# Two paths behind one branch: which block of code lies next to the branch at the end of a segment-attention kernel

## The chip, the cores and the metric

The kernel runs on one core of one Trainium2 chip. A core has five engines with a queue of instructions each: PE (TensorE, matmuls), DVE (VectorE), ACT (ScalarE), POOL (GpSimd) and SP (SyncE, which here only starts transfers). The metric is the device time of one execution in microseconds (us), the median of five runs.

## The reference

16384 tokens of 256 features come with a segment number from 0 to 7 each. Attention runs inside every segment, a linear map follows, then a normalisation of each column over all tokens, a ReLU and the residual. Cut to what matters:

```python
q, k, v = feat @ Wq, feat @ Wk, feat @ Wv          # 32, 32 and 256 columns
starts = jnp.searchsorted(bids, jnp.arange(B))
pos = jnp.arange(N) - starts[bids]
qp, kp, vp = (pad(q), pad(k), pad(v))              # .at[bids, pos].set, 8 x 3072 slots
scores = jnp.einsum('bld,bmd->blm', qp, kp)
scores = jnp.where(mask[:, None, :], scores, NEG)
rp = jnp.einsum('blm,bmd->bld', softmax(scores), vp)
t = rp[bids, pos] @ Wt
tn = (t - t.mean(axis=0)) / jnp.sqrt(t.var(axis=0) + EPS) * gamma + beta
return feat + relu(tn)
```

## The kernel before, in words

The segment numbers of this input are not sorted, so only some tokens own a slot of a segment. The kernel has two paths for this.

The **short path** is `segment_attention_bn_kernel` itself. It holds for segments of at most 768 owners (`FW = FT * P`, six tiles of 128 rows) and for softmax sums within limits. It lists the owners of each segment, gathers their rows, projects them, and attends segment by segment; two switches on the segments' tile counts (L1371) choose the code of each half. From L1403 on it writes the output: sixteen groups of 1024 tokens are read, get the rows of the tokens that own no slot added by matmuls (L1483, L1488) and an add (L1497) or a copy (L1495), and are written by a DMA that ACT starts (L1501). Beside this, POOL writes the owners' rows token by token with indirect DMAs (L1516), in the arms of a third switch (L1529) that POOL alone decides. L1439 to L1441 write `bad`: zero where the short path holds.

The **long path** is `any_lengths` (L41). It computes the whole thing anew for segments of any length, with loops, and stands behind the branch at L1548.

Each engine has its own copy of this control flow. At the end of the short path every engine loads `bad` into a register (L1542) and compares it with zero at L1548. For this input `bad` is zero, so no engine runs the long path. In the compiled order of before, the code of one engine then reads:

```
L1542 TensorLoad bad
L1548 CompareAndBranch
L1548 (the short block: waits, on POOL the counter update, then UnconditionalBranch)
L77 ... L526  any_lengths, ending in L1548 UnconditionalBranch
L1581 the final block
```

The short block is what an engine runs where the long path is not taken. It holds the waits that bring the engines' semaphores to the same state as behind the long path: DVE, ACT and PE wait for their own last instruction and for their load of `bad`; POOL waits for the semaphores of its eight queues of indirect DMAs and then resets them (the ISA instruction, `INC_SWDGE_SEM` in the trace); SP waits for the semaphores of the DMAs that SP and ACT started, the last output groups among them. The unconditional branch at its end leads past the long path into the final block (L1581 in the trace): SP checks all semaphores, every engine drains and reports to a barrier that POOL gathers, the semaphores are cleared, a second barrier follows, and the execution ends.

The trace calls conditional and unconditional branches alike `COMPARE_BRANCH`. On the engines that the change touches, the long path between the short and the final block has 753 instruction rows on PE, 662 on DVE, 396 on ACT, 441 on POOL and 280 on SP (a row can stand for several instructions).

Of the kernel before, what the change touches and what calls it, by code (L numbers as in the profile page):

```python
# [531 lines left out]
def segment_attention_bn_kernel(  # L532
# [44 lines left out]
    with ExitStack() as short:  # L577
# [964 lines left out]
    again = nc.values_load(  # L1542
        bad[0:1, 0:1],
        min_val=0,
        max_val=P * TT + 1,
        skip_runtime_bounds_check_because="a count",
    )
    with tc.If(again > 0, preferred_fallthrough_block=False):  # L1548
        any_lengths(tc, feat, bids, wq, wk, wv, wt, gamma, beta, out)


# [33 lines left out]
```

## Time and profile before

| | us |
|---|---|
| median of 5 runs | 409.54 |
| the five runs | 411.44, 407.35, 412.80, 409.54, 404.53 |
| the profiled execution, its own time | 408.98 |
| its span, first to last instruction | 407.2 |
| mean granted clock of PE in it | 0.779 |
| busy: PE, DVE, POOL, ACT | 292.5, 262.7, 169.1, 109.0 |
| last matmul, as recorded | 389.4 |
| last copy on ACT (L1495), start | 392.7 |
| last output transfer's semaphore, seen by SP | 401.1 |

The page gives shares over the whole span; what the change touches lies in the last 4% of it, so that the views by line and by stretch of time are the ones to read. In them "q" behind an engine's name (POOLq, PEldq) is its sequencer, whose waits, branches and drains are not counted as busy. A line of such a view holds the count of an instruction, its least, median and longest duration in ns, and the start of the first and of the last one in us.

### The profile page before, as it was taken

The page shows a single profiled execution, that of the slowest core. Times are in us where ns is not written, and L with a number is a line of the kernel's source. Part 1 is how long each engine was busy: PE and PEld are TensorE (multiplying, and loading weights), DVE is VectorE, ACT ScalarE, POOL GpSimd, SP SyncE. Part 2 cuts the span into 40 slices and gives each one's busy share as a digit, 9 for nine tenths or more (in the row PEclk, how much of TensorE's full clock was granted, in tenths as well). Part 3 has the DMA queues.
Part 4 walks back from the last instruction along what each step waited for, and adds up shares of the span by engine and source line. Part 5 has one row for each costly group of instructions (what it writes and reads, how often), then busy time and mean ns, then how long its engine had stood idle before and what let it go on. Part 6 is the DMA issues. An engine that isn't in the chain of part 4 may idle for free.

```text
span 407.2 us, 4145 instructions
## 1 busy us (share of the span) xinstructions
PE 292.5 (72%) x1139; PEld 180.0 (44%) x1139; DVE 262.7 (65%) x776; ACT 109.0 (27%) x208; POOL 169.1 (42%) x181
## 2 busy tenths in 40 slices
PE   1669596820599989849798969996596878569920
PEld 0336364510357758616585657763132333123300
DVE  8973799415478853658787236467998975269710
ACT  8414433100333443314213422442011211022100
POOL 3425057778132050067875720000114077743740
PEclk9979699875689999968989989999555555555555
DMA  4101022020211220221032102177799997965642
GB/s 108 39 7 57 2 60 79 22 60 0 77 29 46 78 68 4 82 51 50 18 117 81 42 0 70 22 272 238 277 399 402 386 384 295 346 248 200 263 159 100
DMA packets 20905, 53.34 MB, mean 131 GB/s; under 512 B 6606, under 2 KB 13344, under 8 KB 16746
## 3 DMA queue, kind: packets, MB, share of 16 engines
q1 hardware_dynamic: 11493, 25.06, 17.4%
q10 hardware_dynamic: 2421, 16.83, 10.3%
q0 software_dynamic: 6928, 10.81, 8.8%
q14 instruction: 48, 0.39, 0.4%
q8 instruction: 15, 0.25, 0.3%
HBM read 26.67 MB, written 29.92 MB: 139 GB/s over the span
## 4 chain that ended last, share of the span: by engine, by line
PE 50%; DVE 18%; issue 12%; DMA 8%; another core or an unknown queue 4%; ACT 3%; DVEq 0%; SPq 0%; ACTq 0%
PE po L1008 20%; PE pv L953 8%; PE pf L1488 7%; PE pqk L934 5%; DMA work<-in_r_feat 5%; PE s L967 4%; DMA out<-work 3%; PE px L922 2%; PE pf L1483 2%; DVE work L1497 2%; DVE tk L1013 1%; DVE upto L887 1%; DVE work L941 1%; DVE py L1456 1%
## 5 line engine op out<-in xcount | busy, mean ns | idle before, releaser
L1008 PE MATMUL po<-work 128*128 128x257 f32 x394 | 101.8, 407 | 9.9 <-ACT work L972 4.8
L1008 PEld LDWEIGHTS po<-work 128*128 128x128 f32 x394 | 77.9, 204 | 27.3 <-ACT work L972 6.5
L836 POOL DMA_INDIRECT xs<-in_r_feat,idx x48 | 50.5, 1052 | 79.7 <-issue 40.7
L1516 POOL DMA_INDIRECT out<-tk,idx x48 | 47.3, 985 | 45.5 <-DVE tk L1458 22.1
L836 POOL DMA_INDIRECT reads_r<-reads_of,idx x48 | 53.5, 1115 | 19.3 <-issue 15.0
L953 PE MATMUL pv<-wvt,work 128*128 128x256 f32 x164 | 40.8, 400 | 24.3 <-issue 19.9
L953 PEld LDWEIGHTS pv<-wvt,work 128*128 128x128 f32 x164 | 31.5, 197 | 33.0 <-issue 22.4
L1483 PE MATMUL pf<-y,hot 48*128 48x256 bf16 x128 | 27.7, 390 | 20.1 <-issue 8.4
L1497 DVE TENSOR_TENSOR work<-work,pf 128x512 f32<-128x512 f32 x40 | 26.0, 682 | 23.7 <-remote 13.9
L1488 PE MATMUL pf<-work,ident 128*128 128x256 f32 x64 | 39.1, 714 | 3.1 <-DMA work<-in_r_feat 3.1
L1012 DVE RECIPROCAL rdens<-po 128x1 f32<-128x1 f32 x39 | 6.2, 164 | 52.9 <-PE po L1008 32.7
L972 ACT ACTIVATE work<-s,mask 128x512 f32<-128x512 f32 (+2 forms) x62 | 32.6, 600 | 18.5 <-PE s L967 10.1
L997 ACT ACTIVATE sq<-tk 128x256 f32<-128x256 f32 x39 | 16.3, 417 | 57.9 <-DVE tk L1013 47.1
L1483 PEld LDWEIGHTS <-hot 48*128 48x128 bf16 x128 | 7.2, 104 | 47.4 <-issue 47.3
L967 PE MATMUL s<-work 32*128 32x512 f32 (+2 forms) x124 | 24.9, 597 | 2.8 <-ACT work L972 2.8
L957 ACT COPY work<-pv 128x512 f32<-128x512 f32 (+1 forms) x21 | 12.0, 576 | 48.0 <-remote 21.4
L1495 ACT COPY work<-pf 128x512 f32<-128x512 f32 x16 | 9.4, 585 | 54.7 <-PE pf L1488 38.8
L934 PE MATMUL pqk<-work,wqk 128*128 128x512 f32 (+2 forms) x52 | 23.1, 589 | 0.4 <-issue 0.4
L922 PE MATMUL px<-ident,xs 128*128 128x128 f32 x82 | 15.3, 288 | 9.8 <-issue 4.6
L1488 PEld LDWEIGHTS pf<-work,ident 128*128 128x128 f32 x64 | 16.0, 310 | 12.4 <-issue 9.1
L998 DVE SCALAR_TENSOR_TENSOR acc<-sq,reads_r,acc 128x256 f32<-128x256 f32 x39 | 18.8, 482 | 1.2 <-ACT sq L997 0.7
L1488 PE MATMUL pf<-f,ident 128*128 128x256 f32 x32 | 19.5, 714 | 0.0
(241 smaller groups left out, 371.9 us busy)
## 6 DMA issues: line engine op xcount, KB each, us to landing
work<-in_r_feat SPq DMA_DIRECT2D x14, 1024.0 KB
out<-work ACTq DMA_DIRECT2D x14, 1024.0 KB
t_rows<-tk SPq DMA_DIRECT2D x3, 768.0 KB
t_rows<-tk SPq DMA_DIRECT2D x4, 512.0 KB
f<-in_r_feat SPq DMA_DIRECT2D x2, 1024.0 KB
out<-f ACTq DMA_DIRECT2D x2, 1024.0 KB
eb<-edge_of SPq DMA_DIRECT2D x16, 96.0 KB
t_rows<-tk SPq DMA_DIRECT2D x4, 256.0 KB
```

Source lines behind the costliest of these rows:

```text
L836: nc.gpsimd.indirect_dma_start(out=dst, out_offset=None, in_=table, in_offset=bass.IndirectOffsetOnAxis(ap=ind, axis=0), bounds_check=n - ...
L922: nc.tensor.transpose(px[:, ts(t, P)], xs[:, b * FT + t0 + t, ts(h, P)], ident)
L934: nc.tensor.matmul(pqk[:, 0:w], wqk[:, h, :], xT[:, h, own_c], start=(h == 0), stop=(h == DH - 1),)
L953: nc.tensor.matmul(pv[:, t, :], xT[:, h, ts(t0 + t, P)], wvt[:, h, :], start=(h == 0), stop=(h == DH - 1),)
L967: nc.tensor.matmul(s[:, i, 0:w], k[g, t // 4, :], q[g, c : c + w], start=True, stop=True)
L972: nc.scalar.activation((pr_b if c else pr_a)[:, t, 0:w], s[:, i, 0:w], AF.Exp, bias=mask[:, m : m + 1],)
L998: nc.vector.scalar_tensor_tensor(acc[:, 1, :], sq, reads_r[:, one], acc[:, 1, :], ALU.mult, ALU.add)
L1008: nc.tensor.matmul(po, pr[:, t, ts(r, P)], v[:, t, :], start=(t == 0), stop=(t == T - 1))
L1483: nc.tensor.matmul(pfs[k][:, u, :], hot[r, c, i + u, :], y3[r, :], start=True, stop=not on_pe,)
L1488: nc.tensor.matmul(pfs[k][:, u, :], ident, f_bufs[k % IOB][:, i + u, :], start=False, stop=True,)
L1497: nc.vector.tensor_add(two, two, pfs[k])
L1516: w = nc.gpsimd.indirect_dma_start(out=out, out_offset=bass.IndirectOffsetOnAxis(ap=idx[:, at : at + 1], axis=0), in_=y, in_offset=None, b ...
```

## The change

The order of the blocks behind the branch at L1548 is turned round, and the block gets a name:

```diff
-    with tc.If(again > 0, preferred_fallthrough_block=False):
+    with tc.If(again > 0, preferred_fallthrough_block=True, label="long"):
         any_lengths(tc, feat, bids, wq, wk, wv, wt, gamma, beta, out)
```

The compiled order of one engine becomes:

```
L1542 TensorLoad bad
L1548 CompareAndBranch
L77 ... L526  any_lengths, ending in L1548 UnconditionalBranch
L1548 (the short block: waits, on POOL the counter update, then UnconditionalBranch)
L1581 the final block
```

The instructions themselves and their waits are the same on all five engines; everything ahead of the branch keeps its order.

## The prediction

> **What bounds the kernel now.** I read the chain of waits first, then the end stretch by stretch, then the two lines whose code is rearranged. The chain, cut to 380 us and later:
>
> ```profile
> 386.45 0.58 ACT work L1495
> 387.04 5.65 another core or an unknown queue
> 392.69 0.02 issue
> 392.71 0.58 ACT work L1495
> ```
>
> The last computed thing is a copy on ACT at 392.7, which waited for PE (PE's recorded matmuls end at 389.4, but its semaphore comes at 392.7). Nothing ahead of this is touched, so the change can only move what lies between the first branch of an engine and the end of the span at 407.2. The stretches after 393, with engines' busy time, PE clock, DMA share and GB/s in their last columns:
>
> ```profile
> 393.00:396.00 3.00, 0.00 (x0) 0.00 (x0) 0.00 (x0) 0.30 (x1) 0.25 (x1) 0.50 0.67 254
> 396.00:399.00 3.00, 0.00 (x0) 0.00 (x0) 0.00 (x0) 0.00 (x0) 0.00 (x0) 0.50 1.02 421
> 399.00:402.00 3.00, 0.00 (x0) 0.00 (x0) 0.00 (x0) 0.00 (x0) 0.00 (x0) 0.50 0.13 49
> 402.00:407.20 5.20, 0.00 (x0) 0.00 (x0) 0.00 (x0) 0.00 (x0) 0.00 (x0) 0.50 0.02 5
> ```
>
> The last output groups land by about 401; then 6 us pass in which no engine computes and hardly a byte moves. What fills them stands in the sequencers' lines of the branch (L1548) and of the final block (L1581, cut to 390 us and later):
>
> ```profile
> L1548 SPq EVENT_SEMAPHORE  x9: 17/17/700, 354.9 to 401.3; - x9
> L1548 POOLq EVENT_SEMAPHORE  x6: 17/30/43, 393.8 to 396.5; - x6
> L1548 SPq COMPARE_BRANCH  x2: 33/369/705, 353.4 to 401.4; - x2
> L1548 PEldq COMPARE_BRANCH  x2: 98/1912/3727, 384.7 to 393.0; - x2
> L1548 DVEq COMPARE_BRANCH  x2: 41/52/64, 389.8 to 390.4; - x2
> ...
> L1548 POOLq COMPARE_BRANCH  x2: 38/47/56, 393.7 to 398.1; - x2
> L1548 ACTq COMPARE_BRANCH  x2: 33/44/55, 395.3 to 395.6; - x2
> ...
> L1548 POOLq INC_SWDGE_SEM  x1: 1418/1418/1418, 396.6 to 396.6; - x1
> ```
>
> ```profile
> L1581 SPq EVENT_SEMAPHORE  x14: 17/28/28, 403.9 to 407.1; - x14
> L1581 POOLq EVENT_SEMAPHORE  x4: 17/17/17, 406.4 to 407.1; - x4
> L1581 POOLq DRAIN  x3: 46/109/5137, 401.2 to 406.9; - x3
> L1581 SPq DRAIN  x3: 7/7/7, 404.7 to 406.6; - x3
> L1581 DVEq DRAIN  x2: 10/29/48, 393.6 to 406.6; - x2
> L1581 PEldq DRAIN  x2: 8/36/65, 396.8 to 406.7; - x2
> L1581 ACTq DRAIN  x2: 8/44/80, 401.4 to 406.6; - x2
> ```
>
> Two branches per engine: the first is the comparison, which falls into the short block; the second jumps over the long path. From the second to the first instruction of the final block pass 3.2 us on DVE (390.4 to 393.6), 3.8 on PE (393.0 to 396.8, with the branch's own 3.7), 5.8 on ACT (395.6 to 401.4), 3.1 on POOL (398.1 to 401.2), 2.5 on SP (401.4 to 403.9). A branch into code that is at hand costs far less: POOL's first leads to its first wait in 0.1 us (393.7 to 393.8). So the long jump is a stall of 2.5 to 5.8 us, worst while the output groups move. SP and POOL take theirs after their waits for the DMAs, the others while they'd wait anyway. SP reports to the barrier at 404.7 to 404.8. POOL is last: its drain of 5.1 us runs from 401.2 to 406.3, and the rest takes 407.2 - 406.3 = 0.9.
>
> **The change, part by part.** In the new order the comparison itself makes the long jump, ahead of the waits, and the branch behind the waits is a short one.
>
> DVE, PE: the jump starts 0.6 us earlier on DVE (389.8) and 8.3 earlier on PE (384.7). Both reported at 393.6 and 396.8 and wait for the barrier until 406.5. Worth nothing. If PE's jump held up queued matmuls it would show on ACT, but PE's matmuls were running on from the queue across the branch at 384.7.
>
> ACT: the jump starts at 395.3 instead of 395.6. With the same 5.8 it lands at 401.2; two waits (0.2 from the comparison to the second branch) and a short branch (0.1) give 401.5, against 401.4. It reports some 5 us ahead of POOL's end: cost nothing, and still nothing if POOL gains 3.
>
> SP: the jump starts at 353.4, under the output traffic; its waits then hold it until 401.4 as before. The 2.5 behind them becomes 0.1; its checks in the final block take 403.9 to 404.7, 0.8. It reports at 401.4 + 0.1 + 0.8 = 402.3, 2.5 earlier. SP starts no DMA behind the branch, so nothing is queued behind the jump.
>
> POOL: the jump starts at 393.7 and ends at 393.8 plus its stall. By the range of rows that is 396.3 to 399.6; I take 3.7, PE's row, because PE's jump starts at 393.0, nearest in time and traffic: 397.5. Before, POOL's last waits opened only at 396.4, so 2.6 us of the stall lie under waits that were there anyway and 1.1 sticks out. Then six waits (four took 393.8 to 394.1, two 0.2: 0.5 in all), the counter update (1.4) and the short branch (0.1): the drain begins at 397.5 + 0.5 + 1.4 + 0.1, about 399.6 with the fractions, 1.6 before 401.2. With a stall of 2.5 it would be 398.4 (2.8 earlier); with ACT's 5.8 it is 401.7 (0.5 later).
>
> The unknown is the drain, seen once at this length. The other two on POOL took 0.11 and 0.05 us. I take 5.1 from its start: everything that it could wait for by name was done (POOL's transfers by 396.5, the update by 398.0, output by 401.1), and no other event stands near 406.3. Then POOL ends at 399.6 + 5.1 = 404.7 and the span at 405.6. The bounds: zero, whereupon SP is last (402.3), and an end that hangs on the update instead.
>
> Sum: 407.2 - 1.6 = 405.6 of span, 408.98 - 1.6 = 407.4 for that execution. The median of the runs is 0.6 above it: 407.9. The case's own range is a gain of 2.8 to a loss of 0.5, 406.7 to 410.0 on the median.
>
> Were the second branch no longer at hand when reached (the short block's end and the final block parted by a border of what is loaded), POOL would pay a second stall, 3.1 by its row: 1.5 slower. The two blocks are neighbours and the waits and update last about 2 us, so I only let it widen the range.
>
> The Trainium skill weighs against the whole account: "Advanced Engine Details and Errata", Control Flow Timing, gives about 51 ns for a branch and 108 for a comparison. By these the rearrangement would be worth 0.1 us and the time would stay; the gaps of 2.5 to 5.8 above contradict it for distant targets. And "VectorE: DVE Perf Modes", The DRAIN you can't avoid, calls the drains at a kernel's ends a constant 12 ns or so on all engines; by it SP would set the end and the gain would be that of the third rival below, but POOL's record of 5.1 us differs.
>
> **The rivals.**
>
> *The drain ends a fixed time after the counter update (slower).* The update resets the counters of the queues of 51 indirect DMAs, and the drain's end is 406.3 - 398.0 = 8.3 us after it. If work begun there is what the drain waits for, the time goes by the update's end: 397.5 + 0.5 + 1.4 = 399.4, plus 8.3 is 407.7, a loss of 1.4, or 410.9 on the median; with ACT's stall, a loss of 3.5 (413.0). It turns against the change as soon as POOL's jump takes over 2.3 us (396.6 - 0.5 - 393.8), below every jump seen. For it: the first drains follow no such update and are short. Against: the update is recorded as done.
>
> *The drain ends by something that the change doesn't move.* No difference: 409.5. For it: 5.1 us have no visible cause. Against: I find no event there.
>
> *The drain is short when it begins earlier, or is no work at all.* It would have to shrink below 402.3 - 399.6 = 2.7; then SP's 402.3 plus 0.9 ends the span at 403.2, a gain of 4.0: 405.5. For it: the other two drains. Against: nothing visible held this one back.
>
> **How the numbers follow.** Forecast 0.55, slower by the update 0.20, no difference 0.12, short drain 0.13. All lie between 405.5 and 413.0. The five runs spread by 8.3 us, 2% of the median, which is what a measurement can tell from no change; with a standard deviation of some 3.3 their median is uncertain by 1.25 * 3.3 / 2.24 = 1.8. I add most of that to the shorter cases: 404.2 to 411.4, leaving out the slow end of the first rival. Over 2% either way means 8.2 us: to gain it nearly all behind 399 would have to vanish, to lose it two or three stalls would have to stack on one engine. 0.94 within, 0.03 each side.
>
> **What would show it.** Right: in the lines of L1548 one long gap behind the comparison of each engine, at 354 on SP and 394 on POOL, and the second branch 0.1 before the final block; SP's checks ending 0.9 after its last DMA wait; POOL's drain near 399.6, 5.1 long. A drain still ending 8.3 after the update, or shrunk to less than 2.7, names the rival. Wrong from the ground: a long gap behind the second branch as well, or PE's last semaphore later than 392.7 relative to its matmuls.

## The result and the profile after

| | before | after |
|---|---|---|
| median of the runs, us | 409.26 (94 runs, 401.31 to 421.50) | 406.37 (52 runs, 399.00 to 419.23) |
| the profiled execution, us | 408.98 | 408.30 |
| its span, us | 407.2 | 406.4 |
| mean granted clock of PE | 0.779 | 0.773 |

The ratio after to before is 0.9921 with an interval of 0.9890 to 0.9951: of 409.26 us that is a gain of 3.2 us, between 2.0 and 4.5. It is real, and within 2%. Comparisons set aside disturbed executions, more than 1.5% above a kernel's fastest; as these times spread by 5%, the ratios of the experiments, with some ten runs each, hang on a few runs, and where such a ratio and the medians disagree, both are told.

The two profiled executions differ by 0.8 us of span, a quarter of that gain. They have to be compared piece by piece. First the branch (L1548) in the kernel after; a line has the count, the least, median and longest duration in ns, and the first and last start in us:

```profile
L1548 SPq EVENT_SEMAPHORE  x9: 17/17/17, 361.3 to 403.1; - x9
L1548 POOLq EVENT_SEMAPHORE  x6: 17/30/43, 398.5 to 399.0; - x6
...
L1548 SPq COMPARE_BRANCH  x1: 6/6/6, 356.5 to 356.5; - x1
L1548 PEldq COMPARE_BRANCH  x1: 4870/4870/4870, 385.7 to 385.7; - x1
L1548 DVEq COMPARE_BRANCH  x1: 70/70/70, 392.2 to 392.2; - x1
L1548 POOLq COMPARE_BRANCH  x1: 62/62/62, 395.7 to 395.7; - x1
L1548 ACTq COMPARE_BRANCH  x1: 60/60/60, 397.8 to 397.8; - x1
L1548 POOLq INC_SWDGE_SEM  x1: 1418/1418/1418, 399.1 to 399.1; - x1
```

The long gap now follows the comparison (a jump is counted here from the end of the branch to the engine's next instruction; on PE it is the branch's own time): 395.7 to 398.5 on POOL, 356.5 to 361.3 on SP, 397.8 to ACT's first wait at 403.5, 392.2 to 395.2 on DVE, and 4.9 us on PE. Each engine shows one branch instead of two, so the second has no record in the trace; its cost is read from the final block (L1581, cut to 385 us and later):

```profile
L1581 POOLq DRAIN  x3: 46/109/5052, 400.5 to 406.1; - x3
L1581 SPq DRAIN  x3: 7/7/7, 403.9 to 405.8; - x3
L1581 PEldq DRAIN  x2: 8/8/8, 395.4 to 405.9; - x2
L1581 DVEq DRAIN  x2: 10/14/17, 395.4 to 405.9; - x2
L1581 ACTq DRAIN  x2: 8/8/8, 403.7 to 405.8; - x2
```

POOL's update ends at 399.1 + 1.4 = 400.5 and its drain starts at 400.5, so no stall is left behind the waits. The drain ends at 400.5 + 5.05 = 405.6, and that is again the last thing: SP is ready at 404.0, ACT at 403.7. The end of the chain of waits (start, us, what) has another piece:

```profile
387.97 7.08 another core or an unknown queue
395.05 0.02 issue
395.07 0.59 ACT work L1495
```

ACT's last copy starts at 395.07, 2.36 later than before. The recorded matmuls end at 390.3, 0.9 later, and the copy comes 4.8 after them where it came 3.3 after them in the trace of before. So this execution was behind by 2.4 when its end began, and made up 3.1 from there. ACT's copy isn't the best mark, though, as POOL's last events do not follow from it directly. POOL's last indirect writes, before and after:

```profile
L1516 POOL DMA_INDIRECT out<-L,idx x3: 983/984/984, 389.7 to 392.3; - x3
```

```profile
L1516 POOL DMA_INDIRECT out<-L,idx x3: 985/987/987, 390.6 to 393.2; - x3
```

From the end of the last one (393.25 before, 394.21 after) to the end of the span pass 13.95 and 12.20 us: 1.75 less.

### The profile page after: what moved, and what is told of

Read it like the earlier page. It is cut to its first block, busy times and chain, and to the rows that moved or that the text cites. A ratio compares the mean times of both kernels' runs of the same rounds, so it can differ in the third digit from the quotient of the medians.

```text
span 406.4 us, 4140 instructions
## 1 busy us (share of the span) xinstructions
PE 297.8 (73%) x1139; PEld 183.1 (45%) x1139; DVE 263.2 (65%) x776; ACT 109.3 (27%) x208; POOL 166.9 (41%) x181
## 4 chain that ended last, share of the span: by engine, by line
PE 56%; DVE 17%; issue 10%; another core or an unknown queue 5%; DMA 5%; ACT 3%; ACTq 0%; DVEq 0%; SPq 0%
PE po L1008 24%; PE pv L953 10%; PE pf L1488 7%; PE pqk L934 4%; PE s L967 4%; DMA work<-in_r_feat 3%; PE pf L1483 3%; PE px L922 3%; DMA out<-work 2%; DVE work L1497 2%; DVE tk L1013 1%; DVE py L1456 1%; DVE tk L1458 1%; PE pc L867 1%
## 5 line engine op out<-in xcount | busy, mean ns | idle before, releaser
L1008 PE MATMUL po<-work 128*128 128x257 f32 x394 | 104.6, 415 | 13.0 <-issue 6.4
L1008 PEld LDWEIGHTS po<-work 128*128 128x128 f32 x394 | 79.4, 208 | 31.3 <-issue 10.2
L836 POOL DMA_INDIRECT reads_r<-reads_of,idx x48 | 51.2, 1066 | 20.9 <-issue 15.6
L953 PEld LDWEIGHTS pv<-wvt,work 128*128 128x128 f32 x164 | 32.5, 203 | 28.4 <-issue 22.8
L967 PE MATMUL s<-work 32*128 32x512 f32 (+2 forms) x124 | 26.9, 641 | 2.6 <-ACT work L972 2.6
L922 PE MATMUL px<-ident,xs 128*128 128x128 f32 x82 | 16.4, 302 | 9.4 <-ACT work L945 3.7
L934 PE MATMUL pqk<-work,wqk 128*128 128x512 f32 (+2 forms) x52 | 22.2, 568 | 0.4 <-issue 0.4
```

Of the source, the lines that this page charges most:

```text
L836: nc.gpsimd.indirect_dma_start(out=dst, out_offset=None, in_=table, in_offset=bass.IndirectOffsetOnAxis(ap=ind, axis=0), bounds_check=n - ...
L922: nc.tensor.transpose(px[:, ts(t, P)], xs[:, b * FT + t0 + t, ts(h, P)], ident)
L934: nc.tensor.matmul(pqk[:, 0:w], wqk[:, h, :], xT[:, h, own_c], start=(h == 0), stop=(h == DH - 1),)
L953: nc.tensor.matmul(pv[:, t, :], xT[:, h, ts(t0 + t, P)], wvt[:, h, :], start=(h == 0), stop=(h == DH - 1),)
L967: nc.tensor.matmul(s[:, i, 0:w], k[g, t // 4, :], q[g, c : c + w], start=True, stop=True)
L1008: nc.tensor.matmul(po, pr[:, t, ts(r, P)], v[:, t, :], start=(t == 0), stop=(t == T - 1))
```

## The experiments

The forecast left open what the long jump costs POOL once it stands ahead of the waits, and what the drain's end depends on. The theory is that POOL loses only what of its jump sticks out behind the landing of its last indirect write, and that its drain counts from its own start. The diffs below show the lines that differ from the named kernel, with a line or two around them; "..." marks what is left out.

**The order of before, with POOL late.** Two fills of a tile of 128x768 on POOL, and a copy on DVE that POOL waits for, stand between the last write and the load of `bad`. If the wait opens when a transfer lands, POOL has time to spare there in the old order:

```diff
+    tc.no_sync_barrier()
+    scr = bad_pool.tile([P, FW], F32, name="scr")
+    seen = bad_pool.tile([P, 1], F32, name="seen")
+    for _ in range(2):
+        nc.gpsimd.iota(
+            scr, pattern=[[1, FW]], base=0, channel_multiplier=0,
+            allow_small_or_imprecise_dtypes=True,
+        )
+    nc.vector.tensor_copy(seen, scr[:, 0:1])
+    nc.gpsimd.memset(scr[:, 0:1], 0.0)
+    tc.no_sync_barrier()
     again = nc.values_load(
```

> The order of before, with two iotas of 768 columns on POOL behind its last write, a copy on DVE that reads them and a POOL memset that waits for that copy: POOL reaches its comparison some 2 us later (two iotas of 0.8 us by the row of L701, and two handovers). Theory (POOL's chain ends the span, and its waits for its own DMAs had about 2.3 us of slack in before): the delay lies under these waits; from ACT's last copy to the end of the span 14.5 to 14.9 us as in before (14.5), ratio to before 1.000 to 1.002, POOL's drain about 5.1 us. Rival (POOL's arrival has no slack, and the gain of the change is something else): 16.5 us, ratio 1.005.

Its median is 410.89 (11 runs) against 409.76 (19 runs) of before; the ratio is 0.9823 (0.9768 to 0.9879), which would be a gain, so the times settle nothing. The lines of its branch, L1559 there, cut to 360 us and later:

```profile
L1559 POOLq EVENT_SEMAPHORE  x6: 17/30/43, 392.7 to 396.5; - x6
L1559 POOLq COMPARE_BRANCH  x2: 38/47/56, 392.6 to 398.1; - x2
```

POOL's comparison came 4.8 us after the start of ACT's last copy (1.0 before), and still its last waits opened only at 396.4, over 3 us after the first four: the time to spare is there. The numbers expected from ACT's copy to the end missed (18.9 measured): POOL's writes ended 2 us behind that copy here, half a us behind it in the trace of before. From the last wait to the end of the span pass 10.15 us, 10.67 in before, of which the jump has 2.6 and 3.1.

**The order of after, with POOL late.** The same lines in the kernel after.

> The same delay of some 2 us on POOL in the order of after. Theory: the long jump has taken the place of the waits, nothing covers the delay, and POOL is last: from ACT's last copy to the end 13.0 to 13.5 us (after: 11.3), ratio to before about 0.997. Rival (the gain came from SP's or another engine's earlier report, POOL is not what ends the span): 11.3 to 11.5 us, ratio 0.992.

The ratio is 0.9971 (0.9933 to 1.0008), medians 408.38 (10 runs) and 409.76. The branch, cut to 360 us and later:

```profile
L1559 POOLq EVENT_SEMAPHORE  x6: 17/30/43, 401.0 to 401.4; - x6
...
L1559 POOLq COMPARE_BRANCH  x1: 62/62/62, 396.9 to 396.9; - x1
```

The jump took 4.1 us (396.9 to 401.0); the last write had landed at 400.17, so 0.8 us of it stuck out. From the last wait to the end pass 7.44 us. The tail from ACT's copy was again longer than expected (16.8). By this trace the late POOL costs, in the new order, the part of its jump behind the landing. The times don't confirm it: the interval of this ratio reaches into that of the kernel after.

**The kernel after, once more**, without an edit:

> The changed kernel again, beside the others on the same chip. Theory: ratio 0.990 to 0.995; from ACT's last copy to the end 11.0 to 11.6 us; POOL's jump 2.5 to 3.7 us, its drain 5.0 to 5.1 us from its start. Rival (the drain ends at a fixed time behind the counter update, 8.3 us as in before): its end 8.3 us behind the update, and about no gain.

Medians 406.03 (4 runs) and 409.76; the ratio 0.9829 (0.9756 to 0.9901) rests on too few runs. Its branch (cut to 360 us and later) and its final block (cut to 385 us and later):

```profile
L1548 POOLq EVENT_SEMAPHORE  x6: 17/30/43, 394.8 to 399.1; - x6
...
L1548 POOLq COMPARE_BRANCH  x1: 62/62/62, 391.8 to 391.8; - x1
```

```profile
L1581 POOLq DRAIN  x3: 46/109/5052, 400.7 to 406.3; - x3
```

Here the whole jump (391.8 to 394.8, 3.0 us) lies under the landing: the first four waits pass by 395.1 and the last two open at 399.0. The expected tail from ACT's copy (11.0 to 11.6) missed with 15.4, since the last write landed 5.9 us after POOL had issued it, 0.95 in the first profile of after. The drain is 5.05 us from its start and ends 5.1 after the update's end, where the first rival wants 8.3.

The executions with the long path and all 51 indirect writes side by side, in us. "Landing" is that of POOL's last indirect write, by the semaphore update in the trace; "sticks out" is the part of POOL's jump behind the landing, which in the order of before is all of it:

| execution | POOL's jump | landing | last wait starts | sticks out | last wait to end |
|---|---|---|---|---|---|
| before | 3.1 | 396.41 | 396.52 | 3.1 | 10.67 |
| before, POOL late | 2.6 | 396.40 | 396.51 | 2.6 | 10.15 |
| after | 2.8 | 395.16 | 398.97 | 2.8 | 7.44 |
| after, POOL late | 4.1 | 400.17 | 401.42 | 0.8 | 7.44 |
| after, once more | 3.0 | 399.04 | 399.15 | 0 | 7.44 |
| after, with hints | 5.1 | 390.78 | 391.26 | 0.03 | 7.42 |

Behind the last wait the new order always has 7.4 us: 0.1 of wait, 1.4 of update, 5.05 of drain, 0.85 of barriers; the old one has the jump on top, and a drain longer by 0.085 us. What an execution gains is, by this, the jump less what still sticks out, and less up to 0.4 us: a POOL that comes late out of its jump passes six open waits one after the other, so its last one starts 0.45 us behind the jump, where a POOL that was waiting starts it 0.1 behind the landing. The first profile of after gained nothing by this: its last write had landed before POOL compared at all. In the runs further below with 27 and 3 indirect writes, 4.3 us of a jump of 5.8 and 1.3 of 3.3 stuck out.

**A near target.** Is it the distance, or any taken branch? The long path, which this input doesn't run, is replaced by a few instructions on each engine, in both orders (the diff is against before):

```diff
     with tc.If(again > 0, preferred_fallthrough_block=False):
-        any_lengths(tc, feat, bids, wq, wk, wv, wt, gamma, beta, out)
...    (two small tiles, y and ps, and col, a view of out)
+            nc.sync.dma_start(y, col[:, :, 0])
+            nc.vector.tensor_scalar(y, y, 1.0, None, ALU.add)
+            nc.tensor.matmul(ps, y, y, start=True, stop=True)
+            nc.scalar.copy(y, ps)
+            nc.gpsimd.memset(y, 0.0)
+            for c in range(8):
+                nc.gpsimd.dma_start(col[0:64, :, c], y[0:64, :])
+                nc.sync.dma_start(col[:, :, 8 + c], y)
+                nc.scalar.dma_start(col[:, :, 16 + c], y)
```

> The order of before, with the long path replaced by a handful of instructions on each engine (it isn't run for this input), so that the final block lies a few instructions behind the short block; the waits and POOL's counter update stay. Theory (the cost behind the waits is the distance of the jump): the second branch of each engine leads on within 0.7 us instead of 2.5 to 6.5; from the opening of POOL's last wait to the end of the span 7.5 to 7.7 us instead of 10.2 to 10.8; ratio to before about 0.992, as the change. Rival (a taken branch behind waits costs 2.5 us or more wherever it leads): 10.2 us or more, ratio 1.000.

> The order of after with the same tiny long path. Theory: the comparison now leads on within 0.7 us too; from the opening of POOL's last wait, or from its arrival there, 7.5 us to the end; no more to be had than in the tiny path in the order of before, ratio to before 0.988 to 0.993. Rival (the order of the blocks has a value of its own, besides the distance): clearly less than the tiny path in the order of before.

Old order: median 401.4 (10 runs) against 404.23 of before in the same set (25 runs), ratio 0.9874 (0.9790 to 0.9958): taking away the far target alone gains about what the change gains. Its branch (L1548) and final block (L1595), cut to 360 us and later:

```profile
L1548 POOLq EVENT_SEMAPHORE  x5: 17/43/43, 381.0 to 387.6; - x5
...
L1548 POOLq COMPARE_BRANCH  x2: 38/47/56, 380.9 to 389.1; - x2
...
L1548 SPq COMPARE_BRANCH  x1: 33/33/33, 388.0 to 388.0; - x1
```

```profile
L1595 SPq EVENT_SEMAPHORE  x14: 17/28/28, 389.0 to 395.1; - x14
L1595 POOLq DRAIN  x3: 46/104/5052, 389.3 to 394.9; - x3
```

POOL's second branch leads on in 0.12 us (from its end at 389.14 to the drain's start), ACT's in 0.13, DVE's in 0.16; SP's took 1.0, over the 0.7 expected. From the last wait to the end pass 7.6 us without any change of order. New order: median 399.8 (10 runs), which is 0.989 of before's, but ratio 0.9967 (0.9900 to 1.0035). Its branch, cut to 360 us and later:

```profile
L1548 POOLq COMPARE_BRANCH  x1: 62/62/62, 387.2 to 387.2; - x1
```

POOL's comparison leads on in 0.13 and 7.4 us pass from the last wait. So the stall belongs to the far target, not to the branch, and with a near target the order makes a difference of 0.2 us from the last wait on.

The trace also shows that code is fetched with the far target. It counts the packets that bring instructions (queue, packets, MB, share of the DMA engines); first in before, then with the tiny path in the old order:

```profile
q14 instruction: 48, 0.39, 0.4%
q8 instruction: 15, 0.25, 0.3%
```

```profile
q14 instruction: 40, 0.33, 0.3%
q8 instruction: 13, 0.21, 0.2%
```

The new order has the same two pairs of counts. Ten packets go with the far target. In before, three of these packets start between 399.4 and 399.8, inside POOL's jump (398.1 to 401.2) and ACT's (395.6 to 401.4); with the tiny path the last one starts at 381.1, 8 us ahead of POOL's second branch. Which packet is for which engine isn't shown.

**A hint ahead of the jump.** The kernel after, told on all engines where the branch will go, right ahead of the load of `bad`:

```diff
+    tc.no_sync_barrier()
+    tc.mark_branch_hint_location(
+        "long", 0, engines=(mybir.EngineType.Activation, mybir.EngineType.SP, mybir.EngineType.PE, mybir.EngineType.DVE, mybir.EngineType.Pool,)
+    )
     again = nc.values_load(
```

> The order of after with a prefetch hint for the long jump on every engine, ahead of the load of the flag. Theory: POOL's hint comes only 0.4 us ahead of its branch and ACT's 1.1, so their stalls shrink by no more than that (POOL 2.3 to 3.7, ACT 4.5 to 5.5 us), and where POOL's last wait opens later than POOL arrives, nothing is gained; ratio to before 0.988 to 0.993. Rival (the hint brings the target at once): stalls of 0.7 us or less on all engines and up to 1 us more gained in runs where POOL arrives late.

It missed. Median 400.88 (10 runs) against 404.23, ratio 0.9952 (0.9887 to 1.0016), which is no more than the kernel after gains without it. The branch is L1552 here, cut to 360 us and later:

```profile
L1552 POOLq EVENT_SEMAPHORE  x6: 17/30/43, 390.8 to 391.3; - x6
...
L1552 POOLq COMPARE_BRANCH  x1: 54/54/54, 385.6 to 385.6; - x1
```

POOL's jump took 5.1 us, ACT's 5.8, SP's and PE's 4.6, DVE's 3.1: none is shorter than the shortest seen without a hint. The hint stands under the final block's line in the trace, on POOL:

```profile
L1585 POOLq BRANCH_PREFETCH_HINT  x1: 41/41/41, 385.1 to 385.1; - x1
```

It runs 0.5 us ahead of the comparison on POOL and DVE and 1.1 to 1.2 on the others, less than any far jump took, and the packets of instructions are 48 and 15 as without it. Whether it came too late or doesn't fetch this target wasn't found: no earlier hint was run.

**What sets the drain.** The kernel after, with every second of the 48 token writes left out (half of the owners' rows aren't written), and with all 48 left out (none of those rows is written; three other indirect writes stay):

```diff
-                for at in range(b * FT, b * FT + FT):
+                for at in range(b * FT, b * FT + FT, 2):
```

> The order of after with every second of the 48 indirect writes of L1516 left out (half of the owners' rows are not written), 27 instead of 51. It is for the length of POOL's first drain. Theory (a fixed piece of work behind indirect DMAs, counted from its start): 5.0 to 5.1 us again. Rival one (work per indirect DMA): 5.1 * 27 / 51 = 2.7 us. Rival two (the drain waits for a moment set by the output groups): its end stays 10.5 us behind ACT's last copy, whatever its start.

```diff
                 for at in range(b * FT, b * FT + FT):
-                    put(tk[:, at, :], at, waits[b])
+                    pass
```

> The order of after without the 48 indirect writes of the segments' rows (these rows of the output are not written; the 3 of the list of other tokens stay). For POOL's first drain, 5.05 us behind 51 such writes and 3.09 behind 27. Theory two, formed on these (a fixed part and a part per indirect write, straight line): 3.09 - 24 * 0.082 = 1.1 us. Rival (a part that grows faster than the count, by the DMAs since the last counter update, 90 and 66): below 0.2 us, as the drains without such work.

One run each, 391.45 and 379.08 us. The final block of the first (L1581) and of the second (L1580):

```profile
L1581 POOLq DRAIN  x3: 46/109/3092, 385.3 to 389.3; - x3
```

```profile
L1580 POOLq DRAIN  x3: 40/109/1137, 375.3 to 377.0; - x3
```

The longest drain goes from 5.05 us with 51 indirect writes to 3.09 with 27 and 1.14 with 3. That is a straight line, 0.082 us per write and 0.9 besides, since (5.05 - 3.09) / 24 and (3.09 - 1.14) / 24 agree within 1%. The counter update follows it: 1.42, 0.94, 0.44 us, 0.020 per write. The expectation of a fixed 5 us fell; that of 1.1 us with three writes, made from the first two lengths, held. Every write here has 128 rows, so rows and instructions weren't told apart.

## Why the prediction was right, by its steps

*The second branch is the stall, and it is a matter of the target.* Held: 0.12 us with the tiny path against 2.6 to 3.1 on POOL.

*DVE, PE and ACT are worth nothing.* Held, with less room on ACT than forecast: it is ready at 403.7, 1.9 before POOL's 405.6, not 5. ACT's last copy did come later behind the recorded matmuls (4.8 us against 3.3), which had been named as a sign of a wrong ground. But the same lag is 2.4 to 2.6 us in the three other long-path executions of the new order, and 1.9 in the second one of the old order. It varies with the execution; that PE's earlier jump makes it longer isn't shown.

*SP reports 0.9 after its last wait.* Held: last wait 403.1, ready at 404.0.

*POOL: waits 0.5, update 1.4, a short branch, drain 5.1 from its start, 0.9 to the end.* Held in every execution of the new order with all 51 writes: 0.5, 1.4, below 0.1, 5.05, 0.85. The rivals fell with it. The drain ends 5.1 after the update, not 8.3, and 5.05 did not shrink to less than 2.7; and the interval of the ratio leaves no change out. What the forecast could not know is that the 5.1 is no constant but work in proportion to the indirect writes, most of it.

*"Before, POOL's last waits opened only at 396.4, so 2.6 us of the stall lie under waits that were there anyway and 1.1 sticks out."* This is the term that was mis-sized. With this 1.1 the sum had the gain at 1.6 us, below the measured interval of 2.0 to 4.5. In the four long-path executions of the new order with all writes 2.8, 0.8, 0 and 0 us stuck out (the last by less than 0.05). The step took the cover from one execution, in which the last write landed 3.2 us after POOL had finished issuing it. In the other long-path executions that was 6.7 (old order, POOL late), 6.2, 5.9 and 4.9, and only 0.95 in the profile of after. With the whole jump covered the gain is the 2.6 to 3.1 that the old order pays, and that is near the end of 2.8 which the forecast took for a short stall. The gain of 3.2 agrees with cover that is mostly complete; how often it is can't be read from four traces. The 3.7 us taken for POOL's jump itself lie within the 2.8 to 5.1 measured there. That the forecast for the profiled execution, 407.4, came within 1 us of its 408.30 is luck: its jump had no cover, and it was shorter behind POOL's last write only because that write landed 2.2 us sooner than in before.

The cover goes with the order of ACT and POOL. ACT's last copy releases the last two output groups, and when it starts 1.3 to 2 us before POOL's last indirect write ends, that write lands late, in 4.9 to 6.7 us. When it starts 0.5 before, as in the profile of before, it is 3.2 us, and when it starts 0.9 after, as in the profile of after, 0.95 us. This is read from the traces; no run changed it alone, so that the output groups hold the write up isn't shown.

No version that beats the kernel after was found. The tiny path isn't one: it doesn't compute what longer segments need.

## What to carry to other kernels

Where one side of a branch holds a large body that isn't run, find the engine that ends last and try the jump over that body ahead of its waits for DMAs, not behind them: here it then cost only what stuck out past the landing, and the kernel gained 0.8%. Measure how much cover there is over several executions, because one profile can show all of the jump covered or none of it. And in a kernel with many indirect writes expect a drain at the end that grows with their number, as here from 1.14 us with 3 to 5.05 with 51.

## What was not expected of the hardware

Each indirect write of 128 rows costs about 0.10 us at the very end of the program (0.082 of drain and 0.020 of counter update), beside the 0.98 us that POOL takes to issue it.

The jump over the long path took from 2.6 to 5.8 us on POOL alone (5.8 in the run with 27 writes), and the hint left it at 5.1. The Trainium skill, "Runtime: NRT & Kernel Launch", Instruction fetch mechanics, says that a taken branch to a target outside the window of loaded code has to fetch the code first, and gives no length for that; the near and the far target (0.12 against 2.6 to 3.1 us) and the ten packets of instructions that go with the far one agree with it.
